# Squares through DRAM and VectorE in place of TensorE's transposes, for seven blocks of normed tokens

## The chip, the core and the metric

The kernel runs on one core of a Trainium2 chip. The metric is the device time of one execution in microseconds. The core has a matrix engine (TensorE, PE in the profile; its weight loads have a row of their own, PEld), a vector engine (VectorE, DVE), an activation engine (ScalarE, ACT), GpSimd (POOL), and the queue of SyncE (SP), which issues nearly all of this kernel's DMA transfers. The engines run side by side and wait for each other by semaphores. Each works through its own instructions in order.

## What is computed

One layer: a graph step over 4096 tokens of 256 features, then attention and eight experts. Cut to what the change touches:

```python
# graph step
h = features @ neigh_W.T
h = adj @ h / (adj.sum(axis=1, keepdims=True) + 1.0)
x = x + concatenate([features, h], axis=-1) @ lin_W.T     # features = layernorm(x)
# feed-forward part, first half
h = rmsnorm(layernorm(x)) * ln1_w
q, k, v = h @ wq.T, h @ wk.T, h @ wv.T                    # then rope on q and k, causal softmax, att @ v
...
# second half: router, the best two of eight experts for each token, silu(flat @ w1.T) * (flat @ w3.T) @ w2.T
```

Everything is float32. The projections `h @ wq.T` and so on contract over the 256 features, and TensorE contracts over partitions. So the normed tokens, which VectorE makes with tokens on partitions, have to be turned to have features on partitions first. This turn is what the change is about.

## The kernel before

The tokens are cut into eight blocks of 512, each held as four tiles of 128 tokens. `res[b]` is the residual of block b, with tokens on partitions. `qT[b]` is a piece of 128 partitions by 1024 columns of the tensor `qT_all`, and holds turned data: two halves of 128 features, 512 tokens each. `kT[b]` and `vv[b]` are 128 x 512 each and hold keys and values later.

The first third of the kernel is the graph step. `aggregate(b, steps)` (L510) makes output block b from eight adjacency blocks of 1 MB: a loop over jb = 0 to 7, in which TensorE multiplies adjacency block 8b + jb with the features of token block jb. It does so in seven products of half-size matrices (Strassen's way, L532), each of two matmuls. The sums of quarter blocks that these products need are made by VectorE in `halve` (L489 to L492), one adjacency block ahead. The adjacency blocks stand in a ring of three tiles; `load(n)` (L272) issues the DMA of a block on the SP queue at the end of iteration jb for the block three further on, once TensorE has finished the block whose tile it takes.

The order of the work is written out by hand. `aggregate` calls the functions listed in `steps[jb]` after the fourth of the seven products of iteration jb, and those in `steps[jb, "end"]` after the seventh, just before the load. The projections of block b - 1, whose graph step is finished, are spread in this way over iterations 1 to 5 of `aggregate(b)`, for b = 1 to 7, that is for the seven blocks 0 to 6 (the list at L628):

- jb = 1: `scales` makes mean and variance (VectorE) and the two scale factors (GpSimd). `turn_tables` transposes the rotary tables on VectorE (L311).
- jb = 2: `norm` (L572) writes the four normed tiles into the room of `kT` and `vv` (L174, a helper), and a ratio. `spread_tables` issues three DMAs on the SP queue that copy the tables to three other groups of 32 partitions (L316).
- jb = 3: `turn` (L582) calls `transposed` (L425): eight 128 x 128 transposes on TensorE against an identity (L431) into two PSUM tiles `tr`, and two ScalarE copies of 128 x 512 into `qT[b]` (L433).
- jb = 4: `values_and_logits` (L596) is the first user of the turned tokens: eight matmuls, with slices of `qT[b]` as the stationary operand. Then come two matmuls for the keys (L612), and VectorE multiplies the result with the tables (L619).
- jb = 5: the two query products (L612).

On each engine the order is that of these calls. On VectorE, `halve` for block jb + 1 stands at the head of iteration jb, ahead of the steps of that iteration. On the SP queue, iteration jb = 2 issues the three table copies, then the load of adjacency block 5 of this round.

The last block (7) has projections of its own, which the change does not touch. In the expert third of the kernel, the rows of chosen tokens are fetched from a DRAM list in squares already, four DMAs of 64 KB each with runs of 256 bytes (L1441), and turned by VectorE's transpose (L1490).

Of the kernel before, what the change touches and what calls it, by code (L numbers as in the profile page):

```python
# [9 lines left out]
F32 = mybir.dt.float32  # L10
# [3 lines left out]
ALU = mybir.AluOpType  # L14
# [3 lines left out]
P = 128  # L18
N = 4096
C = 256  # L20
# [46 lines left out]
def fast_kernel(  # L67
# [104 lines left out]
    def normed(dst, b, t, scale):  # L172

        nc.vector.tensor_scalar(  # L174
            dst, res[b][:, t, :], mv[b][:, t, 0:1], scale, op0=ALU.subtract, op1=ALU.mult
        )
# [8 lines left out]
        vv[NB - 1].rearrange("p (r t) c -> p r (t c)", r=2),  # L185
    ]
    m_late = qT_all[:, (NB - 1) * 1024 :][:, 0 : 2 * (C + 1)].rearrange("p (c o) -> p c o", c=2)

    def linear(pool, b, r, banks, m_sb):

# [16 lines left out]
    def ratio(pool, b):  # L207

        r = pool.tile([P, TB, 1], F32, tag="ratio", name=f"ratio_{b}", bufs=1)
        nc.vector.reciprocal(r, both[b])  # L210
        nc.vector.tensor_mul(r, r, rstd[b])
        return r
# [40 lines left out]
    with (  # L253
# [14 lines left out]
        def load(n):  # L268

            if n < NB * NB:  # L270
                blocks[n] = adjs.tile([P, TB, 512], F32, tag="a", name=f"a_{n // NB}_{n % NB}")
                nc.sync.dma_start(blocks[n], adj[n // NB, n % NB])  # L272
# [35 lines left out]
        def turn_tables(b):  # L308

            for k in range(2):  # L310
                nc.vector.transpose(tables[b][0:Q, k, :], tables[b][3 * Q :, k, :])  # L311

        def spread_tables(b):

            for n in range(1, 4):
                nc.sync.dma_start(tables[b][n * Q : (n + 1) * Q], tables[b][0:Q])  # L316
# [193 lines left out]
        def aggregate(b, steps):  # L510

            acc = [
                pool.tile([P, 2, 2 * P], F32, tag="acc", name=f"acc_{b}_{k}")
                for k, pool in enumerate((p_acc0, p_acc0, p_acc1, p_acc1))
            ]
            p = {number: acc[bank][:, at, :] for number, (bank, at) in AT.items()}

            u2 = u4 = neighbours[1][:, 0]
            u3 = neighbours[1][:, 1]
            for jb in range(NB):  # L520
                if b:
                    halve(b * NB + jb + 1)
                m = halves_of.pop(b * NB + jb)
                if jb == 0 and b:
                    load_tables(b - 1)
                for i, (number, left, right) in enumerate(
                    BY_BANK if jb in (0, NB - 1) else PRODUCTS
                ):
                    bank, at = AT[number]
                    for k in range(2):  # L530

                        nc.tensor.matmul(  # L532
                            acc[bank][:, at, :], g[jb][:, right, k, :], m[left][:, k, :],
                            start=(jb == 0 and k == 0 and at == 0),
                            stop=(jb == NB - 1 and k == 1),
                            skip_group_check=True,
                        )
                    if i == 3:
                        if jb == NB - 1:
                            nc.scalar.copy(u2, p[1])  # L540
                            nc.vector.tensor_add(neighbours[0][:, 0], u2, p[2])
                            nc.vector.tensor_add(u2, u2, p[6])
                            nc.vector.tensor_add(u3, u2, p[7])
                        for step in steps.get(jb, ()):
                            step()
                for step in steps.get((jb, "end"), ()):
                    step()
                load(b * NB + jb + 3)
            nc.vector.tensor_add(u4, u2, p[5])
            nc.vector.tensor_add(neighbours[1][:, 0], u4, p[3])  # L550
            nc.vector.tensor_sub(neighbours[0][:, 1], u3, p[4])
            nc.vector.tensor_add(neighbours[1][:, 1], u3, p[5])

        def turn_banks(b, r):
            return (
                p_pj.tile([P, 512], F32, tag="pj", name=f"ph_{b}_{r}"),
                p_tr.tile([P, 2, 2, P], F32, tag="tr", name=f"ph_{b}_{r}_1").rearrange(
                    "p c t i -> p (c t i)"
                ),
            )  # L560

        def qkv(b):

            made = {}

            def scales():
                stats(gx, b)
                var = mv[b][:, :, 1:2]
                power(both[b], var, *BOTH)
                power(rstd[b], var, 1.0, EPS_LN)  # L570

            def norm():  # L572

                made["h0"] = [
                    t.rearrange("p (t c) -> p t c", t=2)
                    for t in (kT[b], vv[b].rearrange("p t c -> p (t c)"))
                ]
                for t in range(TB):
                    normed(made["h0"][t // 2][:, t % 2, :], b, t, both[b][:, t])
                made["ratio"] = ratio(gx, b)  # L580

            def turn():  # L582

                made["hT"] = qT[b]
                transposed(
                    lambda t, c: made["h0"][t // 2][:, t % 2, c * P : (c + 1) * P], made["hT"]
                )

            def values_and_logits():
                for h in range(2):  # L590
                    pj = p_tr.tile([P, 2, 2, P], F32, tag="tr", name=f"pv_{b}_{h}")
                    pj = pj.rearrange("p c t i -> p c (t i)")
                    for i in range(2):
                        at = (2 * h + i) * P
                        for c in range(2):
                            nc.tensor.matmul(  # L596
                                pj[:, i, 0 : NE + P], made["hT"][:, c, at : at + P],
                                wqkv_sb[:, c, QK:], start=(c == 0), stop=(c == 1),
                            )
                    nc.scalar.copy(vv[b][:, 2 * h : 2 * h + 2, :], pj[:, :, NE : NE + P])  # L600
                    for i in range(2):
                        t = 2 * h + i
                        nc.scalar.activation(
                            first_lg[b][:, t, :], pj[:, i, 0:NE], AF.Copy,
                            scale=made["ratio"][:, t],
                        )

            def turned_heads(ms):
                pjs = [p_pj.tile([P, 512], F32, tag="pj", name=f"pq_{b}_{m}") for m in ms]
                for m, pj in zip(ms, pjs):  # L610
                    for c in range(2):
                        nc.tensor.matmul(  # L612
                            pj, wqkv_sb[:, c, m * P : (m + 1) * P], made["hT"][:, c, :],
                            start=(c == 0), stop=(c == 1),
                        )
                for m, pj in zip(ms, pjs):
                    to = kT[b] if m == 2 else qT[b][:, m, :]
                    rot = gx.tile([P, 512], F32, tag="rot", name=f"rot_{b}_{m}", bufs=1)
                    nc.vector.tensor_mul(to, pj, tables[b][:, 0, :])  # L619
                    for n in range(4):  # L620
                        nc.scalar.activation(  # L621
                            rot[n * Q : (n + 1) * Q, :], pj[(n ^ 1) * Q : ((n ^ 1) + 1) * Q, :],
                            AF.Copy, scale=1.0 if n % 2 else -1.0,
                        )
                    nc.gpsimd.tensor_mul(rot, rot, tables[b][:, 1, :])  # L625
                    nc.gpsimd.tensor_add(to, to, rot)

            return [  # L628
                [scales, lambda: turn_tables(b)], [norm, lambda: spread_tables(b)], [turn],
                [values_and_logits, lambda: turned_heads((2,))], [lambda: turned_heads((0, 1))],  # L630
            ]

# [37 lines left out]
        for b in range(NB):  # L672
            if b:

                steps = {0: behind, (0, "end"): at_end}
                behind = []
                for jb, fs in enumerate(qkv(b - 1)):
                    steps[jb + 1] = fs
            aggregate(b, steps)
            at_end = [lambda b=b: [linear(gx, b, r, turn_banks(b, r), m_sb) for r in range(2)]]  # L680
        nc.scalar.copy(m_late, m_sb)
# [4 lines left out]
    with (  # L686
# [201 lines left out]
            for p in range(2):  # L888
                nc.vector.tensor_mul(ys[b, p], ys[b, p], qT[b][:, p, :])


        def in_order(x):
            return x.rearrange("p (g c d) -> p c g d", g=4, c=2)

        def in_groups(x):
            return x.rearrange("p (c g d) -> p c g d", g=4, c=2)

        def inputs(b):

# [1077 lines left out]
        def step():  # L1977
            for f in next(rest, []):
                f()
# [802 lines left out]
```

## Time and profile before

| what | value |
|---|---|
| median of three runs | 1519.21 us (1519.09 to 1520.0) |
| the profiled execution | 1519.28 us, of which 1517.6 us is the span from first to last instruction |
| mean granted TensorE clock | 0.999 |
| L431, the transposes in `turn` | 56 in 410 us of graph step (28 from `kT`, 28 from `vv`) |
| L433, the ScalarE copies behind all transposes of this helper | 30, 587 ns each |
| L174, the normed tiles, VectorE | 28, 405 to 411 ns each |
| one round of `aggregate`, from one set of table copies to the next | 59.7 us |

The span holds everything between the first and the last instruction on the core; the time of the execution is 1.7 us more. In the lists of instructions a row names the engine, the line of the kernel, the operation, the tile written and the tiles read, and how often. A float32 matmul shows as two instructions of each kind (a weight load on PEld and a MATMUL on PE), a transpose as one. A bracket at the end of a row in a timeline gives the idle time ahead of it and what ended that.

### The profile page before, as it was taken

The page shows a single profiled execution, that of the slowest core. Times are in us where ns is not written, and L with a number is a line of the kernel's source. Part 1 is how long each engine was busy: PE and PEld are TensorE (multiplying, and loading weights), DVE is VectorE, ACT ScalarE, POOL GpSimd, SP SyncE. Part 2 cuts the span into 40 slices and gives each one's busy share as a digit, 9 for nine tenths or more (in the row PEclk, how much of TensorE's full clock was granted, in tenths as well). Part 3 has the DMA queues.
Part 4 walks back from the last instruction along what each step waited for, and adds up shares of the span by engine and source line. Part 5 has one row for each costly group of instructions (what it writes and reads, how often), then busy time and mean ns, then how long its engine had stood idle before and what let it go on. Part 6 is the DMA issues. An engine that isn't in the chain of part 4 may idle for free.

```text
span 1517.6 us, 28636 instructions
## 1 busy us (share of the span) xinstructions
PE 1504.7 (99%) x10795; PEld 1109.5 (73%) x10795; DVE 1071.6 (71%) x2223; ACT 553.3 (36%) x991; POOL 564.8 (37%) x649
## 2 busy tenths in 40 slices
PE   9999999999999999999999999999999999999997
PEld 8888888888888643444444444348899999999996
DVE  7864655655756577778879879795676877777872
ACT  2102021121121356565655655653222344343341
POOL 2102122121220422364564553551523464554542
PEclk9999999999999999999999999999999999999999
DMA  6434544544434100001010111029977898999965
GB/s 243 132 121 149 175 143 131 171 143 149 154 138 152 36 2 16 29 33 52 33 43 31 43 44 31 29 67 330 259 188 214 257 268 243 268 267 247 274 155 134
DMA packets 105774, 212.19 MB, mean 140 GB/s; under 512 B 62394, under 2 KB 82106, under 8 KB 91994
## 3 DMA queue, kind: packets, MB, share of 16 engines
q1 hardware_dynamic: 92090, 192.00, 39.0%
q0 software_dynamic: 12720, 17.47, 6.4%
q8 instruction: 87, 1.43, 0.4%
q10 hardware_dynamic: 816, 0.79, 0.2%
q14 instruction: 61, 0.50, 0.1%
HBM read 184.48 MB, written 27.13 MB: 139 GB/s over the span
## 4 chain that ended last, share of the span: by engine, by line
PE 97%; DMA 1%; DVE 1%; POOL 0%; ACT 0%; issue 0%; SPq 0%; POOLq 0%; DVEq 0%
PE acc L532 25%; PE sc L785 15%; PE h L1793 13%; PE y_first L827 5%; PE y_second L827 5%; PE y_third L827 5%; PE ye_y L1847 4%; PE hA L1610 4%; PE ye_y L1750 3%; PE ye_ms L1750 3%; PE pq L612 2%; PE hD L1610 2%; PE pf L503 2%; PE ph L193 2%; PE po L913 1%; PE hB L1610 1%
## 5 line engine op out<-in xcount | busy, mean ns | idle before, releaser
L785 PE MATMUL sc<-qT_all,kT 64*64 64x512 f32 (+3 forms) x2304 | 282.1, 557 | 0.5 <-ACT pt_all L793 0.3
L532 PE MATMUL acc<-a,g 128*128 128x256 f32 x1024 | 244.0, 379 | 0.0
L532 PEld LDWEIGHTS acc<-a,g 128*128 128x128 f32 x1024 | 193.5, 190 | 31.8 <-issue 6.7
L785 PEld LDWEIGHTS sc<-qT_all,kT 64*64 64x64 f32 x2304 | 91.2, 133 | 128.6 <-issue 109.2
L793 ACT ACTIVATE pt_all<-sc 128x1024 f32<-128x1024 f32 (+3 forms) x157 | 148.8, 955 | 96.7 <-PE sc L785 94.2
L1873 POOL DMA_INDIRECT acc_dram<-y,late x40 | 63.3, 1583 | 176.9 <-ACT y L1862 113.5
L532 PE MATMUL acc<-more_sums,g 128*128 128x256 f32 x512 | 126.3, 379 | 0.0
L813 DVE TENSOR_TENSOR late<-late,pt_all 128x1024 f32<-128x1024 f32 (+3 forms) x91 | 106.8, 1174 | 24.3 <-POOL pt_all L795 9.9
L433 ACT COPY qT_all<-tr 128x512 f32<-128x512 f32 x30 | 16.3, 589 | 259.1 <-PE tr L431 259.1
L625 POOL TENSOR_TENSOR rot<-rot,tables 128x512 f32<-128x512 f32 x21 | 33.9, 1613 | 198.7 <-ACT rot L621 158.5
L532 PEld LDWEIGHTS acc<-more_sums,g 128*128 128x128 f32 x512 | 97.2, 190 | 13.2
L827 PE MATMUL y_first<-pt_all,vv 64*64 64x512 f32 (+3 forms) x448 | 106.6, 554 | 0.0
L1793 PE MATMUL h<-late,qT_all 128*128 128x256 f32 (+1 forms) x616 | 104.0, 327 | 0.2 <-DMA qT_all<-in_w_dram 0.2
L827 PE MATMUL y_second<-pt_all,vv 64*64 64x512 f32 (+3 forms) x436 | 104.2, 555 | 0.0
L1793 PEld LDWEIGHTS h<-late,qT_all 128*128 128x128 f32 x616 | 93.5, 191 | 9.9 <-ACT late L1477 1.1
L1075 POOL DMA_INDIRECT lists<-row,slots x64 | 88.4, 1381 | 17.3 <-issue 14.9
L827 PE MATMUL y_third<-pt_all,vv 64*64 64x512 f32 (+3 forms) x372 | 88.7, 555 | 0.0
L1800 DVE TENSOR_TENSOR late<-si,h 128x256 f32<-128x256 f32 (+2 forms) x87 | 39.4, 466 | 65.0 <-ACT si L1799 46.9
L621 ACT ACTIVATE rot<-pq 32x512 f32<-32x512 f32 x84 | 49.5, 589 | 82.6 <-DVE qT_all L619 43.6
L1799 ACT ACTIVATE si<-h 128x256 f32<-128x256 f32 (+2 forms) x87 | 36.0, 418 | 107.4 <-PE h L1793 98.5
L813 DVE TENSOR_TENSOR sum_all<-sum_all,pt_all 128x1024 f32<-128x1024 f32 (+3 forms) x51 | 56.0, 1098 | 15.8 <-POOL pt_all L795 9.5
L793 ACT ACTIVATE late<-sc 128x1024 f32<-128x1024 f32 (+3 forms) x55 | 50.9, 927 | 41.3 <-PE sc L785 37.9
(493 smaller groups left out, 3337.3 us busy)
## 6 DMA issues: line engine op xcount, KB each, us to landing
a<-in_adj_dram SPq DMA_DIRECT2D x64, 1024.0 KB, 4.9
qT_all<-in_w_dram SPq DMA_DIRECT2D x18, 1408.0 KB, 11.6
pt_all<-in_w_dram SPq DMA_DIRECT2D x16, 1408.0 KB, 10.8
res_all<-in_w_dram SPq DMA_DIRECT2D x17, 768.0 KB, 5.5
pt_all<-in_w_dram SPq DMA_DIRECT2D x16, 768.0 KB, 5.5
res_all<-in_w_dram SPq DMA_DIRECT2D x8, 1408.0 KB
qT_all<-in_w_dram SPq DMA_DIRECT2D x9, 768.0 KB, 5.4
late<-lists SPq DMA_DIRECT2D x96, 64.0 KB, 4.6
```

The costliest lines, as they stand in the source:

```text
L532: nc.tensor.matmul(acc[bank][:, at, :], g[jb][:, right, k, :], m[left][:, k, :], start=(jb == 0 and k == 0 and at == 0), stop=(jb == NB - ...
L621: nc.scalar.activation(rot[n * Q : (n + 1) * Q, :], pj[(n ^ 1) * Q : ((n ^ 1) + 1) * Q, :], AF.Copy, scale=1.0 if n % 2 else -1.0,)
L785: nc.tensor.matmul(ps[k * HP : (k + 1) * HP, j, :w], kT[sb][hd, i * P + k * HP : i * P + (k + 1) * HP], qT[b][hd, p, off:], start=True, st ...
L793: nc.scalar.activation(pt[:, :, :w], ps[:, :, :w], AF.Exp, scale=HD ** -0.5)
L813: nc.vector.tensor_add(sums[b, p][:, :, off:], before[:, :, off:], pt[:, :, : 512 - off])
L827: nc.tensor.matmul(accs[b, p][k][hd, off:], vv[sb][some, i, hd], pt[some, j, : 512 - off], start=(s == order_of(b)[0]), stop=(s == order_o ...
L1075: put = nc.gpsimd.indirect_dma_start(out=lists[:, :], out_offset=bass.IndirectOffsetOnAxis(ap=chosen[b][:, k, t, :], axis=0), in_=flats[b] ...
L1610: nc.tensor.matmul(bank[:, n, :], m[left][:, c, :], m[right], start=first and n == 0, stop=True, skip_group_check=True,)
L1750: nc.tensor.matmul(p[number], m[left][:, j, :], m[right][:, j, :], start=(n % 4 == 0 and j == 0), stop=(j == 2), skip_group_check=True,)
L1793: nc.tensor.matmul(ps[m % 2][:, m // 2 - q, :], w13_sb[:, c, m * P : (m + 1) * P], xT[:, c, :], start=(c == 0), stop=(c == 1),)
L1847: nc.tensor.matmul(ps[h if last else 0][:, h, :], hT[:, q, cols], w2_sb[:, q, :], start=(q == 0), stop=(q == NF),)
L1873: put = nc.gpsimd.indirect_dma_start(out=(acc_dram if k < NM - LAST else out)[:, :], out_offset=at, in_=y[:, h, :], in_offset=None, comput ...
```

## The change

The turn of blocks 0 to 6 is done in another way. The normed tiles are written with the features in another order: the 256 features are seen as 2 halves (c) of 4 groups (g) of 32 (d), and stand in the order g, c, d. `leave` writes the two 256 KB halves from `kT` and `vv` to a DRAM tile `turning` on the SP queue. `fetch` reads it back on the same queue in four DMAs of 128 KB, one for each feature group g, into 32 partitions each: partition i of the group takes token 32 m + i for every m, 64 numbers (256 bytes) from each token. Then every 32 x 32 square that has to be transposed stands in 32 partitions, and two VectorE transposes of 128 x 512 (one for each half c) write `qT[b]`. The room for the squares is `qT[b + 1]`, free at that time, or a new tile `last_z` for block 6.

In the order of calls: `leave` comes after `norm` in iteration 2, ahead of the table copies. `fetch` comes in iteration 2 too, after the load, by a new hook `(jb, "loaded")`. `turn` stays in iteration 3, where it now issues the two VectorE transposes and nothing on TensorE or ScalarE. The two helpers `in_order` and `in_groups` existed before (L892) and are moved up.

```diff
@@ aggregate
                 for step in steps.get((jb, "end"), ()):
                     step()
                 load(b * NB + jb + 3)
+                for step in steps.get((jb, "loaded"), ()):
+                    step()
...
+        turning = [tc.dram_tile([512, C], F32, name=f"turning{n}") for n in range(2)]
+        last_z = gs.tile([P, 1024], F32, name="last_z")
+
         def qkv(b):
@@ norm
                 for t in range(TB):
-                    normed(made["h0"][t // 2][:, t % 2, :], b, t, both[b][:, t])
+                    nc.vector.tensor_scalar(
+                        in_order(made["h0"][t // 2][:, t % 2, :]), in_groups(res[b][:, t, :]),
+                        mv[b][:, t, 0:1], both[b][:, t], op0=ALU.subtract, op1=ALU.mult,
+                    )
                 made["ratio"] = ratio(gx, b)
 
+            def leave():
+
+                for n, h0 in enumerate(made.pop("h0")):
+                    nc.sync.dma_start(
+                        turning[b % 2][n * 2 * P : (n + 1) * 2 * P].rearrange(
+                            "(t p) c -> p t c", p=P
+                        ),
+                        h0,
+                    )
+
+            def fetch():
+
+                made["z"] = qT_all[:, (b + 1) * 1024 : (b + 2) * 1024] if b + 2 < NB else last_z
+                squares = turning[b % 2].rearrange("(m i) (g e) -> g i m e", i=Q, g=4)
+                for n in range(4):
+                    nc.sync.dma_start(
+                        made["z"][n * Q : (n + 1) * Q].rearrange("p (m e) -> p m e", e=2 * Q),
+                        squares[n],
+                    )
+
             def turn():
 
                 made["hT"] = qT[b]
-                transposed(
-                    lambda t, c: made["h0"][t // 2][:, t % 2, c * P : (c + 1) * P], made["hT"]
-                )
+                z = made.pop("z").rearrange("p (m c d) -> p c m d", c=2, d=Q)
+                for c in range(2):
+                    nc.vector.transpose(
+                        qT[b][:, c, :].rearrange("p (m i) -> p m i", i=Q), z[:, c]
+                    )
@@ the list of steps
             return [
-                [scales, lambda: turn_tables(b)], [norm, lambda: spread_tables(b)], [turn],
+                [scales, lambda: turn_tables(b)], [norm, leave, lambda: spread_tables(b)],
+                [turn],
                 [values_and_logits, lambda: turned_heads((2,))], [lambda: turned_heads((0, 1))],
-            ]
+            ], fetch
@@ the loop over blocks
-                for jb, fs in enumerate(qkv(b - 1)):
+                made_in, fetch = qkv(b - 1)
+                for jb, fs in enumerate(made_in):
                     steps[jb + 1] = fs
+                steps[2, "loaded"] = [fetch]
             aggregate(b, steps)
```

More of the change, by code (lines that the diff above doesn't have):

```diff
@@ L187, in fast_kernel, with in_order, in_groups @@
     m_late = qT_all[:, (NB - 1) * 1024 :][:, 0 : 2 * (C + 1)].rearrange("p (c o) -> p c o", c=2)
+    def in_order(x):
+        return x.rearrange("p (g c d) -> p c g d", g=4, c=2)
+    def in_groups(x):
+        return x.rearrange("p (c g d) -> p c g d", g=4, c=2)
     def linear(pool, b, r, banks, m_sb):
@@ L889, in normalize @@
                 nc.vector.tensor_mul(ys[b, p], ys[b, p], qT[b][:, p, :])
[L892 to L896, printed above, removed]
         def inputs(b):
```

## The prediction

> **What bounds the kernel now.** I read the page first, then the chain that ended last in the window 80 to 490 us (the rounds in which the changed projections stand), then the timelines of PEld, SP and VectorE around one turn, and last the DMA rates.
>
> ```profile
> span 1517.6 us, 28636 instructions
> PE 1504.7 (99%) x10795; PEld 1109.5 (73%) x10795; DVE 1071.6 (71%) x2223; ACT 553.3 (36%) x991; POOL 564.8 (37%) x649
> PE 97%; DMA 1%; DVE 1%; POOL 0%; ACT 0%; issue 0%; SPq 0%; POOLq 0%; DVEq 0%
> ```
>
> TensorE is the chain, nearly alone: work taken from it shortens the kernel, and a gap put into it lengthens it. In the window:
>
> ```profile
> by line: PE acc L532 80.9%; PE pq L612 8.0%; PE ph L193 5.9%; PE pv L596 3.2%; PE tr L431 1.5%; PE p_bounds L350 0.2%; PE p_wo L376 0.2%; PE tr_wo L366 0.1%
> 105.56 15.54 PE acc L532 x72
> 121.98 6.04 PE acc L532 x28
> 128.02 1.85 PE pv L596 x16
> ```
>
> Start, length, what. Between 105.56 + 15.54 = 121.10 and 121.98 stand the eight transposes of one block: 0.88 us. The share says the same: 1.5% of 410 us is 6.15 us, a seventh of it 0.88. The weight loads show when the turned tokens are first wanted (start, length):
>
> ```profile
> 120.72 0.58 PEld L431 LDWEIGHTS tr<-ident,kT 128*128 128x128 f32 x4
> 121.70 0.73 PEld L532 LDWEIGHTS acc<-a,g 128*128 128x128 f32 x4
> 127.64 2.03 PEld L596 LDWEIGHTS pv<-wqkv_sb,qT_all 128*128 128x128 f32 x16
> ```
>
> The SP queue and VectorE around it:
>
> ```profile
> 112.47 1.94 SPq L316 DMA_DIRECT2D tables<-tables  x3
> 117.68 7.25 SPq L272 DMA_DIRECT2D a<-in_adj_dram  x2
> ...
> 115.86 0.73 DVE L174 TENSOR_SCALAR vv<-res_all,mv,both 128x256 f32<-128x256 f32 x2
> 117.48 0.69 DVE L489 TENSOR_TENSOR qT_all<-a 128x512 f32<-128x512 f32 x1 [0.54 <-DMA a<-in_adj_dram]
> 119.61 0.68 DVE L492 TENSOR_TENSOR a<-a 128x512 f32<-128x512 f32 x1
> 122.60 0.69 DVE L489 TENSOR_TENSOR more_sums<-a 128x512 f32<-128x512 f32 x1 [2.30 <-DMA a<-in_adj_dram]
> ```
>
> The normed tiles are done at 116.59, adjacency block 5 is asked for at 117.68, and VectorE idles from 120.3 to 122.6. The other rounds are the same, 59.7 us later each. The last view is of DMA, where a load (issued 215.47) is followed by the two rotary tables (215.91 and 216.33); columns: stretch, length, clock, DMA share, GB/s.
>
> ```profile
> 216.50:217.00 0.50, 1.00 1.34 180
> 217.00:217.50 0.50, 1.00 0.32 115
> 219.00:219.50 0.50, 1.00 0.85 360
> 219.50:220.00 0.50, 1.00 0.96 188
> 220.00:220.50 0.50, 1.00 0.90 138
> 220.50:221.00 0.50, 1.00 0.02 3
> ```
>
> The load of 1 MB moves until 219.5 at some 400 GB/s, and the tables in runs of 128 bytes only after it, though they were issued 3 us earlier.
>
> **What the Trainium skill says.** "DMA: Bandwidth & Descriptors", section Queues, rings and completion order: each DMA engine consumes a queue's descriptors in ring order. The trace agrees, as just seen. "SBUF — State Buffer", section Door 1: The DMA port swizzle: 32 partitions reach eight of the sixteen ports, about 218 GB/s at best; an estimate from it is 131 KB / 218 = 0.60 us for one fetch of 128 KB and 2.4 us for four. The trace comes near: four fetches of this form, of 64 KB each, moved 142 GB/s at a DMA share of 0.69 (1037 to 1038 us), so 206 at full share. "VectorE: DVE Perf Modes", section The three transpose paths: VectorE's transpose works in 32 x 32 blocks only, which is why the data must come back as squares. "TensorE: Matmul & The Clock Gate", section Part 4: PE-mode transpose, gives some 275 ns for one transpose in a kernel; the trace has 272 to 273. But eight cost 0.88 us, not 8 x 0.27, since they overlap.
>
> **The change, part by part** (block 0's round; the sum is for seven).
>
> Removed: the eight transposes, 0.88 us of the chain, 6.2 us in seven rounds. Of ScalarE two copies of 587 ns that only these projections wait for. Without them TensorE comes to the first projection at 127.64 - 0.88 = 126.76.
>
> Added on that path: TensorE's first projection now waits for two VectorE transposes, and these for four fetches. Step by step:
> - `leave` needs the second pair of normed tiles, 116.59. The new pattern costs nothing: L902 has the same patterns and size, 409 ns against 407. Two issues at 0.38 us (the like write, `acc_dram<-res_all`, took 0.365 to 0.46) end at about 117.0.
> - The three table copies, issued at 112.47 before, now stand behind `leave`. They take 1.94 us of SP: 118.95. Only then load 5, 1.3 us late.
> - `fetch` waits on SP for `leave` to land. 512 KB to DRAM landed in 2.9 us at `acc_dram<-res_all`, so by 119.5; SP would be there at 119.3. Four issues of 512 runs, as the tables' two (0.37 and 0.48), about 0.45 each, end at 121.3. Queued behind is load 6, due at about 124.6, so SP is free for it.
> - Data: the load that the tables followed moved until 4.0 us after its issue (215.47 to 219.5); load 5 thus until 122.95. Behind it 524 KB in runs of 256 bytes at 206 GB/s, 2.55 us: 125.5. The second table landed 216.33 + 5.1 = 221.4, some 0.9 after its last packets: squares landed at 126.4.
> - VectorE: idle since 119.8, so it starts at once, say 126.5. A transpose of 128 x 512 took 0.703 us at L1490; two in a row about 1.35 (the table pair of 32 x 512 took 1.30). The first is done near 127.2, the second near 127.85, seen by TensorE at 127.9.
> - TensorE needs the second half two weight loads after the first, 126.76 + 2 x 0.127 = 127.0. Gap 0.9 us against 0.88 saved: +0.05 us per round, +0.3 us in seven.
>
> At nothing: `halve` of block 5 is queued behind the transposes on VectorE. It starts at 127.9 instead of 122.6 and ends by 130.9; TensorE wants its sums at 135.53, so up to some 5 us of delay is covered, and the key product that L619 waits for comes at 131.6. The table copies land late too (before 125 by their 5.7 us), but L619 is their first user. Load 6 shares DMA with the squares for under 1 us and has until about 134. Were these covers gone, each us would count seven times.
>
> Sum: 1519.28 (its own execution) + 0.3 = 1519.6; the median of the runs is 0.07 lower, which changes nothing.
>
> Unknown, from both sides: the landing of the squares. Early end: if the squares use the engines' slack in the first 1.5 us of the load (share 0.32 at 217.0) or SP passes faster, 125.4, and TensorE doesn't wait: -6.2 us. Late end: load 5 meets the table copies just ahead of it. Load 4, with the copies beside it, landed 5.8 us after its issue (111.64 to 117.48) against the 4.9 median: +0.9; and at 170 GB/s the squares need 0.5 more: a gap of 2.3, +10 us. I take the middle because ring order is seen in the trace, and the rates are measured on the same form.
>
> **Rivals.**
> - All hidden: gap near 0, 1513.1 us; with a gap under 0.45 still faster than 0.2%. For it: seven small margins (issue times, last packets, 0.9 us of landing) were taken without optimism, and 1 us less makes it true. Against: the squares are queued behind a 1 MB load, and ring order holds.
> - A new wait replaces the old work: load 5 is slowed by the table copies as load 4 was, the squares land at 127.3, the gap is 1.85, +0.97 per round, +6.8: 1526. It decides from a landing at about 126.8 on, where the loss passes 3 us. For it: the 5.8 us of load 4. Against: the copies now end before load 5's bulk moves.
>
> That the turn would stay on TensorE can be excluded: the seven pairs of rows L431 from `kT` and `vv` are gone from its list.
>
> **How the numbers follow.** A measurement of this kernel can tell about 0.2% (3 us) from no change. Forecast, the gap cancels the gain: 0.38, own range 1516.5 to 1522.5. All or mostly hidden: 0.34. The new wait wins: 0.28. Chances: faster 0.34, same 0.38, slower 0.28. The range reaches from near full hiding to the loss of the second rival, 1513.2 to 1525.5; one in ten is left out on each side.
>
> **What would show it.** In the changed profile: no L431 after 80 us; TensorE's idle before the first projection near 0.9 us a round, ended by VectorE's transpose; load 5 issued about 1.3 us later; the squares landing 7 us after their issue began; `halve` of block 5 behind the transposes without TensorE waiting for it. It is wrong if there is no idle (the squares came early), if the idle is 2 us or more, or if TensorE waits for sums.

## The result, and the profile after

The changed kernel takes 1528.37 us (four runs, 1527.81 to 1530.97) against 1519.15 before: a ratio of 1.0063, with a 95% interval of 1.0045 to 1.008. It is slower by some 9 us, where no change had been forecast. The profiled execution took 1530.97 us.

The page of the changed kernel, its first lines:

```profile
span 1529.3 us, 28602 instructions
PE 1505.8 (98%) x10739; PEld 1107.0 (72%) x10739; DVE 1081.2 (71%) x2237; ACT 545.2 (36%) x977; POOL 564.4 (37%) x649
```

The 56 transposes are gone (10795 - 10739). The span is 11.7 us longer all the same, so TensorE stands still somewhere. The waits of TensorE, with the total in us, the times and the longest, begin with

```profile
PE pv L632 <- issue: 7.6, 6, 1.7
PE pv L632 <- DVE qT_all L621: 2.5, 1, 2.5
```

All of it is ahead of the first projection (now L632), which waits for VectorE's transpose (L621). The row "issue" is the same wait, seen one step earlier: its weight load had to wait. In the second round, the weight loads of TensorE (start, length, idle before):

```profile
189.20 0.84 PEld L538 LDWEIGHTS acc<-qT_all,g 128*128 128x128 f32 x4
191.70 0.30 PEld L632 LDWEIGHTS pv<-wqkv_sb,qT_all 128*128 128x128 f32 x2 [1.66 <-issue]
192.28 1.69 PEld L632 LDWEIGHTS pv<-wqkv_sb,qT_all 128*128 128x128 f32 x14 [0.28 <-DVE qT_all L621]
```

Without a wait the first projection would load its weights 0.86 us after 189.20 and come to the second half of the features 0.33 us later (127.64 to 127.97 in the kernel before), at 190.39; it gets there at 192.28. I call this difference the gap: 1.9 us. The length of the round agrees. The same four loads of the next round start at 249.90, 60.70 us after 189.20, where a round without transposes and without a gap takes 59.70 - 0.88 = 58.82. Read in the same way, the seven gaps are 3.1, 1.9, 1.7, 2.2, 1.9, 2.3 and 1.2 us, 14.3 in all. The saved transposes give back 6.2, which leaves 8.1.

The SP queue and VectorE of the same round:

```profile
179.91 0.38 SPq L599 DMA_DIRECT2D turning<-vv  x1
180.33 1.80 SPq L322 DMA_DIRECT2D tables<-tables  x3
182.18 0.58 SPq L278 DMA_DIRECT2D a<-in_adj_dram  x1
182.93 2.13 SPq L611 DMA_DIRECT2D qT_all<-turning  x4
...
190.92 1.30 DVE L621 STREAM_TRANSPOSE qT_all<-qT_all 128x512 f32<-128x512 f32 x2 [7.92 <-DMA qT_all<-turning]
192.15 0.65 DVE L495 TENSOR_TENSOR more_sums<-a 128x512 f32<-128x512 f32 x1
```

Load 5 goes out when the forecast had it, 2.3 us after the normed tiles (179.89). The squares land 8.7 us after that, and VectorE has idled for 7.9. (In the first round the issue of the second write took 0.97 us in place of 0.38, and load 5 went out at 119.77, 0.8 us later than forecast; its gap is the longest.) `halve` of block 5 comes late behind them (192.15), and nobody waits for it. The DMA rates between (stretch, length, clock, share, GB/s):

```profile
182.50:183.00 0.50, 1.00 0.94 221
183.50:184.00 0.50, 1.00 0.91 164
184.50:185.00 0.50, 1.00 0.93 393
186.00:186.50 0.50, 1.00 1.01 426
187.50:188.00 0.50, 1.00 1.41 168
188.00:188.50 0.50, 1.00 1.36 161
```

Until 182 the writes are moving and until 184 the table copies. The bulk of load 5 moves from 184 to 186.75, and the squares then crawl at some 165 GB/s, until load 6 joins them at 189; they end by 190.

Most of the rest of the 11.7 us in this execution is clock. In the sixth round (stretch, length, TensorE's busy time, clock, share, GB/s):

```profile
434.00:436.00 2.00, 0.84 (x5) 1.00 0.79 332
436.00:438.00 2.00, 2.00 (x15) 0.67 0.03 8
438.00:440.00 2.00, 2.00 (x4) 0.50 0.00 0
```

After the gap TensorE is busy, but at half the granted clock. The same happens in the first round. From the first projection's weights to the second pair of products after it, these rounds take 5.85 and 6.35 us where the second takes 4.67: 1.2 and 1.7 us lost. 8.1 + 2.9 = 11.0 us of the 11.7; the other 0.7 lies outside these rounds, and its place isn't known.

### The profile page after: what moved, and what is told of

The parts are those of the page before. It is cut to its first block, busy times and chain, and to the rows that moved or that the text cites. A ratio compares the mean times of both kernels' runs of the same rounds, so it can differ in the third digit from the quotient of the medians.

```text
span 1529.3 us, 28602 instructions
## 1 busy us (share of the span) xinstructions
PE 1505.8 (98%) x10739; PEld 1107.0 (72%) x10739; DVE 1081.2 (71%) x2237; ACT 545.2 (36%) x977; POOL 564.4 (37%) x649
## 5 line engine op out<-in xcount | busy, mean ns | idle before, releaser
L636 ACT COPY vv<-pv 128x256 f32<-128x256 f32 x14 | 5.2, 372 | 268.0 <-PE pv L632 268.0
L538 PE MATMUL acc<-qT_all,g 128*128 128x256 f32 x256 | 65.7, 379 | 0.0
```

The source lines that it names most:

```text
L538: nc.tensor.matmul(acc[bank][:, at, :], g[jb][:, right, k, :], m[left][:, k, :], start=(jb == 0 and k == 0 and at == 0), stop=(jb == NB - ...
```

## The experiments

Theory 1: the wait for squares that move behind load 5 costs the time. Its rivals are contention of the added traffic, the way through DRAM as such, and the granted clock.

**The fetches ahead of load 5.**

```diff
-                steps[2, "loaded"] = [fetch]
+                steps[2, "end"] = [fetch]
```

> The four fetches are issued ahead of load 5 (hook "end" in place of "loaded"); nothing else changes. Theory 1, the wait for squares queued behind the 1 MB load: the fetches go out as soon as leave has landed, move at once and land some 4 us earlier than in the changed kernel (about 187 instead of 190.9 in the second round), the transposes are done before TensorE comes, no gap, and the whole 6.2 us is gained: about 1513 us. Load 5 then comes about 2.5 us later than in the changed kernel, with some 5 us to spare. Rival, the way through DRAM itself takes too long (write, receipt, read in runs of 256 bytes): the gap stays above 1 us a round and the time near 1527. Rival, load 5 becomes the late one: TensorE waits for sums of halve, over 1519.

1513.97 us (1513.38 to 1514.56), ratio to before 0.9964 (0.995 to 0.9977). SP, VectorE and the weight loads in the second round:

```profile
178.02 1.97 SPq L611 DMA_DIRECT2D qT_all<-turning  x4
180.04 12.49 SPq L278 DMA_DIRECT2D a<-in_adj_dram  x3
...
183.81 1.30 DVE L621 STREAM_TRANSPOSE qT_all<-qT_all 128x512 f32<-128x512 f32 x2 [5.24 <-DMA qT_all<-turning]
187.43 0.69 DVE L495 TENSOR_TENSOR more_sums<-a 128x512 f32<-128x512 f32 x1 [2.31 <-DMA a<-in_adj_dram]
...
184.78 0.84 PEld L538 LDWEIGHTS acc<-qT_all,g 128*128 128x128 f32 x4
185.64 2.03 PEld L632 LDWEIGHTS pv<-wqkv_sb,qT_all 128*128 128x128 f32 x16
```

The projections follow the products without a gap, in all seven rounds, and a round takes 58.82 us (184.78 to 243.60). Now VectorE waits 2.3 us for load 5, and TensorE does not notice. One line moved turns the loss of 9 us into a gain of 5.4: the way through DRAM fits, if it starts in time, and the later load is covered. Theory 1 holds, and the rivals fall except as shares.

**The copies behind the fetches.** `leave`, load 5, fetches, table copies.

```diff
-                [scales, lambda: turn_tables(b)], [norm, leave, lambda: spread_tables(b)],
+                [scales, lambda: turn_tables(b)], [norm, leave],
...
-                steps[2, "loaded"] = [fetch]
+                steps[2, "loaded"] = [fetch, spread]
```

> The three table copies go behind the fetches on the SP queue: leave, load 5, fetch, copies. Load 5 is then issued about 1.8 us earlier than in the changed kernel, at its old time. Theory 1 (queue order): squares land 1.8 us earlier or a little more, the gap of about 2 us a round falls to 0 to 0.3, and the time to 1513 to 1516 us. Rival (the reading of the squares, not what stands ahead of it): the gap falls by less than 0.7 us a round, time above 1523. The copies land later; if the key product's first user waits for them, it shows as idle of VectorE and perhaps of TensorE.

1517.12 us (21 runs, 1516.03 to 1521.24), ratio 0.9988 (0.9982 to 0.9995). In the second round:

```profile
177.38 0.35 SPq L278 DMA_DIRECT2D a<-in_adj_dram  x1
178.69 2.15 SPq L611 DMA_DIRECT2D qT_all<-turning  x4
...
186.72 0.30 PEld L632 LDWEIGHTS pv<-wqkv_sb,qT_all 128*128 128x128 f32 x2 [0.28 <-issue]
187.25 1.69 PEld L632 LDWEIGHTS pv<-wqkv_sb,qT_all 128*128 128x128 f32 x14 [0.23 <-DVE qT_all L621]
```

Load 5 is back at its old time. Of the gap some 0.5 us is left, and the kernel is a little faster than before. So the three table copies ahead of the load, 1.8 us of SP and 0.4 MB of traffic, made most of the difference between a small gain and the loss; SP's time and the traffic were not told apart. The gap is up to 0.9 us in other rounds, 3.5 us in all seven. The time is about 1 us above what was expected.

**The fetches on ScalarE's queue.** `nc.scalar.dma_start` in `fetch`, nothing else.

> The four fetches are issued by ScalarE's queue in place of SP's, at the same place in the program; the load and the copies stay on SP. If only the ring order behind load 5 held the squares back, they now share the engines with the load, land some 2 us earlier than in the changed kernel (about 189 in place of 190.9 in the second round), and the load somewhat later: 1514 to 1519 us. If bandwidth and short runs hold them back, whatever the queue, the gap stays near 2 us and the time near 1528.

1527.49 us (1525.15 to 1528.8), ratio 1.0051 (1.0035 to 1.0066): as bad as the change.

```profile
181.85 2.36 ACTq L611 DMA_DIRECT2D qT_all<-turning  x4
...
190.77 1.30 DVE L621 STREAM_TRANSPOSE qT_all<-qT_all 128x512 f32<-128x512 f32 x2 [8.36 <-DMA qT_all<-turning]
```

The fetches leave 0.2 us after the load (181.64), on a queue of their own, and still land 8.9 us later. So it is not the order of one queue that holds them back, as the forecast had it. The DMA view of 184.5 to 186 us, while load 5 (q1) and the squares (q10) are both under way, gives each queue's packets, MB and share of the DMA engines:

```profile
q1 hardware_dynamic: 71, 0.58, 94.4%
q10 hardware_dynamic: 67, 0.02, 5.0%
```

The two queues move nearly the same number of packets, but a packet of the load has 8 KB and one of the squares 256 bytes. Four other rounds show the same (90 to 82, 74 to 70, 70 to 62 and 89 to 87); in the first and the sixth the load was moving alone or nearly so (103 to none, 79 to 9). So beside the load the squares got next to nothing until it was through. The Trainium skill says in "DMA: Bandwidth & Descriptors", section Issuing engines are not separate DMA queues, that transfers started by several engines run on the same sixteen and interleave; this run agrees.

**The gap filled.** Twelve transposes of the identity ahead of the projection, 1.45 us by the trace.

```diff
             def values_and_logits():
+                fill = p_tr.tile([P, TB, P], F32, tag="tr", name=f"fill_{b}")
+                for n in range(12):
+                    nc.tensor.transpose(fill[:, n % TB], ident, ident)
```

> The changed kernel with twelve more transposes of the identity on TensorE just ahead of the first projection (about 1.3 us of work in each of the seven gaps, nobody reads it). Theory 2, the gap costs more than its length since the granted clock falls to half for a while after some gaps (two stretches of 3.4 us in the profile, some 1.5 us lost each): with the gap partly filled the clock stays, and the time falls by what those drops cost, to about 1526 to 1527 us, at a spread between runs below 1 us. Rival, only the length of the wait counts: the time stays where the changed kernel is, 1528.4 us, and the drops appear as before.

1529.94 us (1527.55 to 1533.7), ratio 1.0071 (1.0057 to 1.0085). Over the whole graph step of the profiled run, one row of windows, with TensorE's busy time and then the clock:

```profile
80.00:500.00 420.00, 415.94 (x1959) 1.00 0.53 164
```

The clock stays at 1.00, yet this execution took 1530.41 us. Its waits are longer: measured in the same way, with the fill inside, they are 16.1 us in all, against 14.3. In the fifth round the squares came so late that TensorE idled for another 2.2 us behind the fill; why they came later there is not known. So the clock isn't the cause of the loss; what it adds to a typical run can't be read from these times, because the landing of the squares varies as much.

**The traffic alone.** The kernel before, with `leave` and `fetch` added at their places and TensorE's transposes kept; the squares go to `last_z` in every round, and nobody reads them.

> The kernel before with TensorE's transposes kept, and leave and fetch added at the places of the change, into a room that nobody reads (so this work is extra and its data unused). Theory 1: traffic and later issue of copies and load 5 are covered, only the wait for the squares costs: 1519 to 1519.5 us. Rival, contention: the added 1 MB a round delays loads or copies that TensorE needs, and several of the 9 us appear here: above 1521.

1519.77 us (13 runs, 1519.04 to 1523.25), ratio 1.0005 (0.9996 to 1.0013): no change. No wait of TensorE shows up in the graph step. Contention as a cost of its own falls; counted from the second write (176.18), the second round has the issue times of the changed kernel, load 5 at 178.44 and the fetches at 179.13. Nobody waits for them, and nothing is lost.

**Both moves.** Fetches, load 5, copies.

> Both moves together: leave, fetches, load 5, table copies. The fetches alone ahead of load 5 gave 1513.97 us with no gap left, so the copies' place can give no more: 1513 to 1514.5 us. If it is clearly lower, the copies cost something that I don't see; if higher, they come late for their user.

1514.09 us (1513.28 to 1515.16), ratio 0.9968 (0.9956 to 0.998). As expected, no more than the fetches alone.

**A wait of known length.** The kernel with the fetches first, in which VectorE writes the transposed pair twice, and four times:

```diff
-                for c in range(2):
+                for c in list(range(2)) * 2:
```

> The kernel with the fetches ahead of load 5, and VectorE writes the pair of transposes twice (the same values again), so that TensorE's first projection waits for a known length: 1.3 us less the room that each round had (0.3 to 1.7 us by its trace), about 1.7 us of gap in seven rounds. Only the length counts: 1513.97 + 1.7 = 1515.7 us. The clock falls even after short gaps: above 1518.

> As the one before, with the pair written four times: 3.9 us less the room, gaps of 2.2 to 3.6 us, 19 us in seven rounds. Only the length counts: 1513.97 + 19.2 = 1533 us, no drop of the granted clock in the graph step. A gap of over 2 us also drops the clock to half for 3.4 us: up to 1.6 us more a round, 1537 to 1544 us, with stretches of half clock behind the gaps.

Twice: 1513.93 us (1513.53 to 1514.96). Only the first round has a gap to speak of, 0.8 us; the room was larger than I had worked out, and the time cannot be told from the kernel without the repeat. Four times: 1531.82 us (1530.03 to 1532.54), ratio 1.008 (1.0065 to 1.0096). The gaps in its trace are 3.2, 2.9, 2.0, 2.3, 2.3, 2.1 and 1.4 us, 16.2 in all, and 1514.0 + 16.2 = 1530.2, against 1531.8 measured. So a wait ahead of the projection costs its length, with nothing but VectorE to blame. But two rounds ran at half clock behind the gap, the first and the sixth (stretch, length, TensorE's busy time, clock, share, GB/s):

```profile
132.00:134.00 2.00, 2.00 (x10) 0.50 0.00 0
194.00:196.00 2.00, 2.00 (x15) 1.00 0.02 8
438.00:440.00 2.00, 2.00 (x10) 0.52 0.05 12
```

The second round had a gap of 2.9 us and kept its clock, the sixth had 2.1 and lost it. The length of the gap alone doesn't decide.

**Long runs.** The traffic alone, but read back by one DMA in runs of 1 KB:

```diff
-                for n in range(4):
-                    nc.sync.dma_start(
-                        made["z"][n * Q : (n + 1) * Q].rearrange("p (m e) -> p m e", e=2 * Q),
-                        squares[n],
-                    )
+                nc.sync.dma_start(
+                    made["z"].rearrange("p (t c) -> p t c", c=C),
+                    turning[b % 2].rearrange("(t p) c -> p t c", p=P),
+                )
```

> The kernel with the traffic alone (TensorE's transposes kept, what comes back is unused), but with the 512 KB read back by one DMA into 128 partitions in runs of 1 KB in place of four into 32 partitions each in runs of 256 bytes. Behind load 5 the squares took about 3.2 us to move, at some 165 GB/s, where the prediction had 2.55. If the short runs into few partitions set that, the same bytes now move in 1.3 to 1.7 us, at over 300 GB/s. If reading what was just written to DRAM is slow in itself, the rate stays below 200 GB/s. The time stays at 1519 to 1520 us in both cases.

One run, 1520.81 us (1519.92 for one run of the kernel before beside it). Behind load 5 the read back moved at

```profile
183.00:183.50 0.50, 1.00 0.85 297
183.50:184.00 0.50, 1.00 1.05 354
184.00:184.50 0.50, 1.00 0.99 348
```

some 330 GB/s. The traffic alone is the kernel to compare it with. There the squares moved in the same round, behind load 5, at

```profile
183.50:184.00 0.50, 1.00 1.31 255
184.00:184.50 0.50, 1.00 1.31 262
```

some 260 GB/s. So what was just written can be read back fast, and the form of the squares, 256 bytes into 32 partitions at a time, costs a part of the rate. The two parts of the form (run length, number of partitions) were not told apart. Nor does the form explain the 165 GB/s of the changed kernel, which reads in the same form as the traffic alone. One difference is the room: `qT[b + 1]` in the changed kernel, `last_z` in both of these. The seventh round of the changed kernel writes to `last_z` too, and has its shortest gap, 1.2 us; whether the room matters was not tried.

## Why the prediction was wrong

Point by point:

- What bounds the kernel, the 0.88 us per round and the 6.2 us in all: right. With the gap removed a round takes 58.82 us in place of 59.70, and the kernel is 5.4 us faster.
- The chain of the new wait, step by step, and that TensorE would wait for VectorE's second transpose: right, and the trace shows no other wait. The issue of load 5 came out within 0.1 us in the second round (0.8 us late in the first, the one that the forecast was worked out for), the two transposes at 1.30 us for 1.35, and the landing 0.9 us after the last packets. The second half of the features is wanted 0.33 us after the first and not 0.25, which makes the forecast's own gap 0.8 us.
- The step that failed is the data step, "load 5 thus until 122.95. Behind it 524 KB in runs of 256 bytes at 206 GB/s, 2.55 us: 125.5". Its first term was sized from a load that went out on idle engines; here the 0.4 MB of table copies were still moving, and the bulk of load 5 ended 4.6 us after its issue in place of 4.0. Its second term came from four fetches in the expert third at a DMA share of 0.69 and was scaled up to full share; in the changed kernel 3.2 us was measured, some 165 GB/s. In this form the traffic alone reached 260 GB/s, so 206 is neither a bound nor a rate to count on, and what sets the rate stays open. Together the two terms put the landing some 1.2 us too early a round, so a gap of 1.9 us in the second round and 2.0 on average, not 0.9. The sum over the rounds is 14.3 us in place of some 6.5.
- What was not in the sum at all: the clock. It cost 2.9 us in the profiled execution, on two of seven rounds.
- The covers priced at nothing (`halve` behind the transposes, load 6, the copies): right, and e5's 1.0005 shows the traffic and the moved issues to be free.
- The rival "a new wait replaces the old work" is what happened, with its place and its price per round (1.85 us forecast). It had a chance of 0.28, and the range stopped at 1525.5, inside its outcome. The late end was in the text, a gap of 2.3 and +10 us. The two terms that failed were both taken from other places of the kernel, and both delay the same landing: the sum should have been taken nearer to the late end.
- Ring order, which carried the middle value, was not needed: on another queue the squares land just as late. While the load moved there, the squares' packets were no more in number than the load's, and a 32nd in size.

## What to carry to other kernels

A trip through DRAM that replaces work on the engine that bounds must start early enough to land with everything that moves beside it, not behind one load on idle engines. Before removing such work, look at which transfer of the queue has slack and let the new one go first: here swapping two issues made 14 us of difference. Half a megabyte in runs of 256 bytes did not overtake a 1 MB load here, whichever queue issued it: when two queues moved nearly the same number of packets, the one with small packets moved few bytes.

## What was not expected of the hardware

- Gaps of 2 to 3 us on TensorE sometimes halve its granted clock for 3.4 us (1.2 to 1.7 us lost), and sometimes don't: 3.1 and 2.3 us did in the changed kernel and 2.2 did not; 3.2 and 2.1 did with the repeated transposes and 2.9 did not. The Trainium skill, "TensorE: Matmul & The Clock Gate", section Why this matters for your kernels, warns of gaps of more than about 3 us; here shorter ones were enough in some rounds.
- In these traces the clock changed on a fixed grid of 3.413 us. In the changed kernel the two stretches at half clock are these (stretch, length, TensorE's busy time, clock, share, GB/s):

```profile
129.48:132.90 3.42, 3.04 (x13) 0.50 0.22 91
436.68:440.10 3.42, 3.42 (x11) 0.50 0.00 0
```

  They start 36 and 126 times 3.413 us after the first clock record of the trace, at 6.60. With the repeated transposes they start at 130.90 and 438.10, 37 and 127 times 3.413 after the first record at 4.60, and are as long. So where a gap lies on this grid can matter. It isn't the idle time in one step of the grid alone: TensorE was busy for 1.64 us in the step ahead of the second drop, and for 1.53 us in a step (430.82 to 434.23) of the run with the fetches on ScalarE's queue, which no drop followed. What decides was not found.
- 512 KB in runs of 256 bytes into 32 partitions at a time moved at some 165 GB/s behind a load in the changed kernel and at 260 in the traffic alone, and in runs of 1 KB into 128 partitions at some 330.
- Two DMA queues that were busy at once moved about as many packets each in five of seven rounds, such as 71 of 8 KB and 67 of 256 bytes in 1.5 us.
